# Making layer 1's masks, constant rows and first keys inside layer 0, with per-group slots and a second load of x in layer 0

## The chip, the core and the metric

The kernel runs on one core of a Trainium2 chip. The metric is the device time of one execution in microseconds (us); lower is better. Engines are named as in the profile: PE is the matrix engine (PEld its weight loads), DVE the vector engine, ACT the scalar engine, POOL the GpSimd engine, SP the queue that issues nearly all transfers (SPq in the timeline).

## The reference

Sixteen batches (B = 16) of 512 tokens with 256 features pass through two layers.

- Layer 0 attention: layer norm of x, queries from x, keys and values from the context; 16 heads of 16 features, rotary positions, and each query sees the 65 context positions that end at its own. Softmax, output projection, added to x.
- Layer 0 feed-forward: a gated recurrence over the batches (`c = f*c + i*g`, with gates from the normalized x of the batch and from `c`), sixteen steps, one for each batch. Its result is `h = tanh(x_n @ wo.T + c_final @ uo.T + bo)`, so every batch needs the state after the last one. `x = x + h`.
- Layer 1 attention: layer norm of x, full attention of 512 queries over 1601 context positions with a mask row for each batch. `x = x + attention`.
- Layer 1 feed-forward: eight experts, two for each token with limited room, a 256-1024-256 network with exact gelu.

```python
x = x + L0_xattn(layernorm(x), ctx, ctx)
x = x + L0_ffn(layernorm(x))       # recurrence over the 16 batches, then h for all
x = x + L1_xattn(layernorm(x), ctx, ctx, mask)
x = x + L1_ffn(layernorm(x))       # experts
```

## The kernel before

All tensors are fp32. The program has three blocks, one behind the other: layer 0 (`l0`), layer 1's attention (`l1`), the experts (`l2`). In each block the order of instructions is written by hand: every piece of work is put in a list by `at(when, fn, ...)`, the list is sorted by `when`, and the functions are called in this order. Each engine, and SP, then works through its own instructions strictly in this order; semaphores that the framework sets make it wait for what an instruction needs. A tile has `bufs` buffers that are used in turn, and a new tile waits until the old content of its buffer is no longer read. When a block ends, its tile pools are released and the next block's pools take over that memory.

**Layer 0** (lines 128 to 573). One step of the list is one unit of `when`; a batch takes `T0 = 32` steps, and batch b starts at `s0 = 32*b`. Pieces of several batches lie side by side: loads of batch b at s0-60, key and query projections at s0-49 to s0-35, rotation (`rope`, on POOL, then stores to DRAM in a layout with 32 rows per head) at s0-46 to s0-32. `slot` loads keys (s0-32) and queries (s0-26) back as four head groups at once, in halves `m` of two groups. For each head group g, `maxima` finds row maxima (s0-14+8g), `shift` brings their negatives through DRAM into a spare row of the query tile (s0-8+8g), `scores` and `values` follow (s0+8g). With `s1 = s0+32`, `recip_a` (s1+3) and `recip_b` (s1+6) send the softmax denominators and their reciprocals through DRAM (`raw_d` to `den`, `rec_d` to `rb`), `divide` (s1+10, POOL), `out_proj` (s1+13), `stats` and `finish` (normalization, s1+17), `turn` (transposes, s1+21), `gate` (s1+25) and `step` (s1+36) follow. `add_bias` (POOL, s0-40) adds the folded output bias to the batch's x tile, which is held in one of four buffers from load to `finish`. After the last job `uo` is applied to the final state (L559) and the bias row is added with a one-row matmul (L566).

**Layer 1 attention** (lines 576 to 1280). First the weights are loaded (L586), then constant rows are written into the DRAM tensors `ke_d` and `qe_d` (L621, L624), then the mask is loaded, turned into a keep row and a bias row and stored (L626 to L644). Then a loop over steps n from -84: a batch has `PER = 52` steps (4 head groups x 13 key chunks). `score` and `value` run from n = 0; `max_pair` (row maxima, PE L913 and DVE L921) runs `LEAD = 18` steps ahead. The keys of batch b are made ahead of it: `mask_rows`, `load_k`, `project_k` (PE L801, DVE L808), `mean_k`, `fill_k` (POOL L833), `add_k` (DVE L845), `halve_k` (L851, and L745/L748, which split the keys into a high and a low part), `store_k` (L857). For batch 0 these steps lie at n = -81 to -29, together with `load_x` (L691), `hidden` (L702), `stats`, `norm2`, `turn`, `project_q` (L755) and `store_q` (L770, L772), all of batch 0; the first `max_pair` of batch 0 needs `load_ks` (L893) and `load_qs` (L897), which read what these stored.

Of the kernel before, what the change touches and what calls it, by code (L numbers as in the profile page):

```python
# [2 lines left out]

# [8 lines left out]
F32 = mybir.dt.float32  # L12
# [45 lines left out]
def tile_kernel(ctx: ExitStack, tc: tile.TileContext, a, out):  # L58
# [68 lines left out]

    with ExitStack() as l0:
# [14 lines left out]

        def load(b):
            ctxT = pool.tile([P, 2, S], F32, name="ctxT")
            nc.sync.dma_start(out=ctxT, in_=a["ctxT"][b, :, :, 0:S])
            x_t = pool.tile([P, NQ, D], F32, name="x_t", bufs=4)
            nc.sync.dma_start(out=x_t, in_=a["x"][b])
            state[b] = {"x": x_t, "ctx": ctxT}
# [12 lines left out]
        zero = wp.tile([P, S], F32)  # L162
# [15 lines left out]
        wo0 = weight("wo0", [P, 2, D])  # L178
        gates = weight("gates", [P, 6, 2, D])
        uo = weight("uo", [P, 2, D])  # L180
        bo = wp.tile([P, D], F32)
# [7 lines left out]
        def clear(c):  # L189
            nc.sync.dma_start(  # L190
                out=flat[:, 2 * c * DS : 2 * (c + 1) * DS],
                in_=empty.rearrange("p r d -> p (r d)"),
            )

# [26 lines left out]
        def turn(key, b, k):  # L221
            if k == 0:
                state[b][key] = pool.tile([P, 2, S], F32, name=key)
# [50 lines left out]
        def slot(b, what, m):  # L274
            if m == 0:
                state[b][what] = pool.tile([P, NG, S], F32, name=f"{what}T")
            t_d = (k_d if what == "k" else q_d)[b % 2]
            nc.sync.dma_start(
                out=state[b][what][:, 2 * m : 2 * m + 2, :],
                in_=t_d[2 * m : 2 * m + 2].rearrange("g p n -> p g n"),  # L280
            )
# [23 lines left out]
        def maxima(b, g, half):  # L305
            qT, kT = state[b]["q"], state[b]["k"]
# [4 lines left out]
            for i in range(2):  # L311
                q = 2 * half + i
                lo = WIN if q == 0 else 0
                for j in range(4):
# [3 lines left out]
                        lhsT=qT[r0 : r0 + 32, g, q * P : (q + 1) * P],  # L318
                        rhs=kT[r0 : r0 + 32, g, q * P - WIN + lo : (q + 1) * P],
# [19 lines left out]
        def shift(b, g):  # L339
# [8 lines left out]
                out=state[b]["q"][HD:P:32, g, :],  # L348
# [7 lines left out]
        def scores(b, g, half):  # L356
            qT, kT = state[b]["q"], state[b]["k"]
            sc = [head_tile() for j in range(4)]
            for i in range(2):
                c = 2 * half + i  # L360
                w = width_of(c)
                for j in range(4):
# [3 lines left out]
                        lhsT=kT[r0 : r0 + 32, g, c * P : (c + 1) * P],  # L366
                        rhs=qT[r0 : r0 + 32, g, c * P : c * P + w],
# [41 lines left out]
        def recip_a(b):  # L409
# [5 lines left out]
            comp = pool.tile([P, 2, S], F32, name="comp")  # L415
# [91 lines left out]
        for b in range(B):  # L507
# [3 lines left out]
            for m in range(2):  # L511
                at(s0 - 49 + 2 * m, project, b, "k", m)
                at(s0 - 46 + 2 * m, rope, b, "k", m)
                at(s0 - 32 + m, slot, b, "k", m)
# [3 lines left out]
                at(s0 - 26 + m, slot, b, "q", m)  # L518
# [4 lines left out]
            at(s0 - 40, add_bias, b)  # L523
            for g in range(NG):
                for half in range(2):
# [6 lines left out]
            at(s1 + 6, recip_b, b)  # L532
            at(s1 + 10, divide, b)
            for p in range(2):
                at(s1 + 13 + 2 * p, out_proj, b, p)
# [11 lines left out]
        for c in range(E * CAPP // P // 2):  # L547
            at(7 * c, clear, c)
        jobs.sort(key=lambda x: (x[0], x[1]))
# [4 lines left out]
        for p in range(2):  # L554
            ps = bank()
            for i in range(2):
                q = 2 * p + i
                for k in range(2):
# [5 lines left out]
                        stop=False,  # L564
                    )
                nc.tensor.matmul(  # L566
                    ps[:, i * D : (i + 1) * D],
                    lhsT=one_row,
                    rhs=rows[:, RFO : RFO + D],
                    start=False,  # L570
                    stop=True,
                )
            nc.vector.tensor_copy(cu[:, 2 * p : 2 * p + 2, :].rearrange("p q d -> p (q d)"), ps)


    with ExitStack() as l1:
# [12 lines left out]
        wfo = weight1("wfo", [P, 2, D])  # L589
        wq1 = weight1("wq1", [P, 2, D])  # L590
        wk1 = weight1("wk1", [P, 2, D])
# [3 lines left out]

        ke_d = [dram.tile([NG, P, SKP], F32, name=f"ke_d{i}") for i in range(2)]  # L600
        qe_d = [dram.tile([NG, P, S], F32, name=f"qe_d{i}") for i in range(2)]
        ks_d = [dram.tile([H // 2, P, SKP], F32, name=f"ks_d{i}") for i in range(2)]
        qs_d = [dram.tile([H // 2, P, S], F32, name=f"qs_d{i}") for i in range(2)]
        raw_d = [dram.tile([NG, P, S], F32, name=f"raw1_d{i}") for i in range(2)]
        rec_d = [dram.tile([H, S], F32, name=f"rec_d{i}") for i in range(2)]
        m_d = dram.tile([B, SKP], F32, name="m_d")
        mb_d = dram.tile([B, SKP], F32, name="mb_d")
        rcnt = wp.tile([P, B], F32)
        bo = wp.tile([P, D], F32)


        with tc.tile_pool(name="mask", bufs=1) as mp:
            mask_i = mp.tile([B, SKP], I32)
            nc.sync.dma_start(out=mask_i, in_=a["mask"])
            kf = mp.tile([P, SKP], F32)
            nc.gpsimd.tensor_copy(kf, cols[:, KROW : KROW + 1].to_broadcast([P, SKP]))
            qf = mp.tile([P, S], F32)
            nc.gpsimd.tensor_copy(qf, cols[:, QROW : QROW + 1].to_broadcast([P, S]))
            for t in ke_d:
                for g in range(NG):  # L620
                    nc.sync.dma_start(out=t[g], in_=kf)  # L621
            for t in qe_d:
                for g in range(NG):
                    nc.sync.dma_start(out=t[g], in_=qf)  # L624
            keep = mp.tile([B, SKP], F32)
# [901 lines left out]
```

## Time and profile before

| | us |
|---|---|
| median of 3 runs (5949.54 to 5960.73) | 5958.36 |
| the profiled execution, its own device time | 5928.76 |
| span in the profile | 5926.7 |
| PE busy | 5555.2 (94%) |
| DVE busy | 3412.7 (58%) |
| ACT busy | 2632.9 (44%) |
| POOL busy | 1709.7 (29%) |
| last matmul of layer 0 starts | 1313.1 |
| first `max_pair` of layer 1 starts | 1461.3 |
| first `score` of layer 1 starts | 1535.7 |

The profile is one execution. Times in it are counted from the start of its span, and "busy" is time in which an engine runs an instruction. In a line of the timeline the columns are: start, duration, engine, line of the kernel, operation, output<-inputs by the program's names, shapes, xcount; in brackets the idle time of the engine before it and what ended that.

### The profile page before, as it was taken

How to read it: one execution, taken by the hardware profiler on the slowest of the kernel's cores; microseconds unless marked ns; L12 is line 12 of the kernel's file. 1: busy time of each engine (PE TensorE's matmuls, PEld its weight loads, DVE VectorE, ACT ScalarE, POOL GpSimd, SP SyncE). 2: the span in 40 equal slices, each digit the busy share in tenths (PEclk: the TensorE clock that was granted, in tenths of full speed). 3: DMA queues.
4: the chain of work that ended last, by engine and by line, in shares of the span. 5: the costliest groups of instructions: out<-in, count | busy, mean ns of one | idle time of the engine just before them, and what ended most of it. 6: DMA issues, size and time to landing. Idle time of an engine off the chain costs nothing. (4 is left out here: it accounts for less than half of the span.)

```text
span 5926.7 us, 95832 instructions
## 1 busy us (share of the span) xinstructions
PE 5555.2 (94%) x36560; PEld 2746.7 (46%) x36560; DVE 3412.7 (58%) x9204; ACT 2632.9 (44%) x5250; POOL 1709.7 (29%) x1322
## 2 busy tenths in 40 slices
PE   7999999963999999999999999999999987999999
PEld 4555555531433343333343334334334334766776
DVE  4555555522777777777777777777777741111111
ACT  3444444420355555555555555555555551222121
POOL 4555555322112222122122222313212012222222
PEclk7899898876899999999999999999999998999999
DMA  4333333324454555445445455544544412222211
GB/s 162 118 116 110 114 116 116 104 89 160 139 186 161 171 168 174 169 157 187 151 165 193 160 174 171 172 162 157 185 151 165 132 58 79 69 77 70 65 62 46
DMA packets 343773, 797.92 MB, mean 135 GB/s; under 512 B 46109, under 2 KB 124113, under 8 KB 341138
## 3 DMA queue, kind: packets, MB, share of 16 engines
q1 hardware_dynamic: 324114, 743.72, 37.3%
q0 software_dynamic: 19200, 48.08, 2.3%
q8 instruction: 288, 4.72, 0.3%
q14 instruction: 171, 1.40, 0.1%
HBM read 471.09 MB, written 326.73 MB: 135 GB/s over the span
## 5 line engine op out<-in xcount | busy, mean ns | idle before, releaser
L921 DVE TENSOR_REDUCE pm<-m 128x1 f32<-128x402 f32 (+1 forms) x4096 | 2125.8, 569 | 625.8 <-PE m L913 605.5
L1160 ACT ACTIVATE pt<-e 128x512 f32<-128x512 f32 (+1 forms) x3328 | 1715.9, 602 | 1155.4 <-PE e L1151 1154.2
L913 PEld LDWEIGHTS m<-ks,qs 64*128 64x128 f32 x4096 | 465.9, 186 | 1370.8 <-DVE pm L921 862.4
L913 PE MATMUL m<-ks,qs 64*128 64x402 f32 (+1 forms) x4096 | 1031.3, 452 | 17.2 <-DVE pm L921 14.7
L1151 PE MATMUL e<-qe,ke 32*128 32x512 f32 x6656 | 980.2, 643 | 0.0
L1173 PE MATMUL pv<-pt,vt 128*32 128x256 f32 (+2 forms) x9656 | 976.6, 476 | 0.0
L1354 ACT ACTIVATE hT<-h,cols 128x384 f32<-128x384 f32 (+1 forms) x320 | 199.2, 623 | 753.9 <-PE h L1346 736.3
L1374 PE MATMUL y<-w,hT 128*128 128x256 f32 x2176 | 476.3, 379 | 0.0
L1346 PE MATMUL h<-xeT,w 128*128 128x384 f32 (+1 forms) x1280 | 475.6, 530 | 0.0
L328 DVE CUSTOM_DVE_ANT_0 tmp<-s,cst 128x192 f32<-128x192 f32 (+1 forms) x1024 | 278.9, 336 | 320.1 <-PE s L316 318.9
L1374 PEld LDWEIGHTS y<-w,hT 128*128 128x128 f32 x2176 | 410.4, 190 | 54.4
L1151 PEld LDWEIGHTS e<-qe,ke 32*128 32x128 f32 x6656 | 271.2, 179 | 259.9 <-issue 220.6
L379 DVE TENSOR_TENSOR pt<-s,cst 128x384 f32<-128x384 f32 (+2 forms) x768 | 248.6, 392 | 178.4 <-PE s L364 178.4
L1346 PEld LDWEIGHTS h<-xeT,w 128*128 128x128 f32 x1280 | 243.8, 191 | 213.4 <-issue 114.9
L380 ACT ACTIVATE pt<-pt 128x384 f32<-128x384 f32 (+2 forms) x768 | 244.5, 390 | 190.2 <-DVE pt L379 189.9
L1173 PEld LDWEIGHTS pv<-pt,vt 128*32 128x32 f32 (+1 forms) x9656 | 191.4, 108 | 247.0 <-issue 245.0
L1386 POOL DMA_INDIRECT out<-y_t,xe x136 | 135.1, 994 | 590.8 <-DVE y_t L1383 586.0
L1331 DVE COPY xeT<-tp 128x384 f32<-128x384 f32 (+1 forms) x80 | 45.2, 606 | 446.4 <-PE tp L1328 446.4
L801 PE MATMUL m<-ck,wk 128*128 128x400 f32 (+1 forms) x512 | 215.0, 545 | 90.0 <-DMA ck<-in_ctxT 84.4
L1132 POOL DMA_INDIRECT slots<-row,put x128 | 132.9, 1039 | 571.9 <-issue 477.2
L833 POOL TENSOR_SCALAR u<-m_bc,kmean 128x802 f32<-128x802 f32 x64 | 192.0, 3000 | 327.6 <-DVE kmean L824 308.1
L106 POOL TENSOR_TENSOR rs<-mo,mhalf 128x4 f32<-128x4 f32 x64 | 66.4, 1038 | 691.7 <-DVE mo L104 691.5
(189 smaller groups left out, 5534.0 us busy)
## 6 DMA issues: line engine op xcount, KB each, us to landing
ks<-ks_d SPq DMA_DIRECT2D x128, 802.0 KB
ks_d<-khi SPq DMA_DIRECT2D x128, 401.0 KB
ks_d<-klo SPq DMA_DIRECT2D x128, 401.0 KB
ke<-ke_d SPq DMA_DIRECT2D x64, 802.0 KB
raw_d<-raw SPq DMA_DIRECT2D x128, 256.0 KB
qs<-qs_d SPq DMA_DIRECT2D x64, 512.0 KB
ck<-in_ctxT SPq DMA_DIRECT2D x64, 402.0 KB
ke_d<-kc SPq DMA_DIRECT2D x64, 401.0 KB
```

What stands on the lines that cost most here:

```text
L328: nc.vector.tensor_tensor_reduce(out=tmp[:, lo:], in0=sc[j][:, i, lo:BW], in1=band[:, lo:], scale=1.0, scalar=NEG, op0=ALU.add, op1=ALU.ma ...
L379: nc.vector.tensor_tensor(t, sc[j][:, i, 0:w], c, ALU.min)
L380: nc.scalar.activation(t, t, AF.Exp)
L801: nc.tensor.matmul(ps[:, 0:n], lhsT=wk1[:, k, m * P : (m + 1) * P], rhs=ck[:, k, 0:n], start=(k == 0), stop=(k == 1),)
L913: nc.tensor.matmul(sc[:, 0:n], lhsT=qs[r0 : r0 + 64, jp, q * P : (q + 1) * P], rhs=ks[r0 : r0 + 64, k0 : k0 + n], start=True, stop=True,)
L921: nc.vector.tensor_reduce(pms[b, g][:, q, 2 * jp + jj, part : part + 1], sc[:, 0:n], AX.X, ALU.max)
L1151: nc.tensor.matmul(sc[0:kn, :], lhsT=kt[r0 : r0 + 32, c * P : c * P + kn], rhs=qt[r0 : r0 + 32, :], start=True, stop=True,)
L1160: nc.scalar.activation(pt[0:kn, :], sc[0:kn, :], AF.Exp)
L1173: nc.tensor.matmul(pv[32 * j : 32 * j + 32, part], lhsT=vts[c // 2][0:kn, c % 2, v0 : v0 + 32], rhs=probs[b, g, c, j][0:kn, part], start=f ...
L1346: nc.tensor.matmul(ps[:, 0:n], lhsT=weights[e][0][:, k, m * P : (m + 1) * P], rhs=xeT[:, k, 0:n], start=(k == 0), stop=(k == 1),)
L1354: nc.scalar.activation(hT[:, m, 0:n], ps[:, 0:n], AF.Gelu, bias=cols[:, at : at + 1])
L1374: nc.tensor.matmul(ps[:, 0:D], lhsT=hT[:, m, t * P : (t + 1) * P], rhs=weights[e][1][:, m, :], start=(m == 0), stop=(m == NH - 1),)
```

## The change

Three things are done. (1) `ke_d`, `qe_d`, `ks_d`, `qs_d`, `m_d`, `mb_d`, `rcnt` and the weights `wk1`, `wfo`, `wq1` are made at the top of the kernel, so that layer 0 can use them. In layer 0's list, `masks` makes the mask rows at step 0 (on 64 partitions instead of 16), `constant_rows` writes the constant rows at steps 12 to 96, and the first batch's keys are made at steps 460 to 514 with the functions of `key_pieces`, which layer 1 uses for the other batches. (2) Memory in layer 0: `slot` loads each head group by itself at s0-20+8g, with four buffers of one group for keys and queries each, the x tile has two buffers and is loaded a second time at s1+7, with `add_bias` behind it at s1+11, and `xT`, `x1T`, `comp` and `zero` have fewer buffers. (3) Smaller ones: the bias of `uo` is added by DVE from a broadcast row (`b_out`) instead of four one-row matmuls, layer 1's `fold_bias` goes into its list at -61.5, and layer 1's value tiles are cleared on POOL instead of DVE.

The functions of `key_pieces` are those of layer 1 before, renamed; only what differs is shown.

```diff
+    first_weights = [const.tile([P, 2, D], F32, name=f"{n}_w") for n in ("wk1", "wfo", "wq1")]
+    def key_pieces(pool, bank, bufs):
+        def mask_rows(b):                      # before: m_bc
+            st[b, "keep"] = pool.tile([P, SKP], F32, name="keep", bufs=1)
+            nc.sync.dma_start(out=st[b, "keep"], in_=m_d[b : b + 1, :].to_broadcast([P, SKP]))
+        def load(b, m, i):                     # before: ck, [P, 2, 402]
+            c0, n = parts[i]
+            ck = pool.tile([P, 2, S], F32, name="ctxT")
+            nc.sync.dma_start(out=ck[:, :, 0:n], in_=a["ctxT"][b, :, :, c0 : c0 + n])
...
     with ExitStack() as l0:
+        def load_x(b):
+            x_t = pool.tile([P, NQ, D], F32, name="x_t")
+            nc.sync.dma_start(out=x_t, in_=a["x"][b])
+            state[b]["x"] = x_t
         def load(b):
             ctxT = pool.tile([P, 2, S], F32, name="ctxT")
             nc.sync.dma_start(out=ctxT, in_=a["ctxT"][b, :, :, 0:S])
-            x_t = pool.tile([P, NQ, D], F32, name="x_t", bufs=4)
-            nc.sync.dma_start(out=x_t, in_=a["x"][b])
-            state[b] = {"x": x_t, "ctx": ctxT}
+            state[b] = {"ctx": ctxT}
+            load_x(b)
...
         wo0 = weight("wo0", [P, 2, D])
+        for w, name in zip(first_weights, ("wk1", "wfo", "wq1")):
+            nc.sync.dma_start(out=w, in_=a[name])
...
+        b_out = wp.tile([P, D], F32)
+        nc.sync.dma_start(out=b_out, in_=a["rows"][:, RFO : RFO + D].to_broadcast([P, D]))
...
+        krow = wp.tile([P, SKP // 4], F32)
+        nc.gpsimd.tensor_copy(krow, cols[:, KROW : KROW + 1].to_broadcast([P, SKP // 4]))
+        (qrow likewise)
+        def constant_rows(i, g):
+            for t_d, row in ((ke_d, krow), (qe_d, qrow)):
+                nc.sync.dma_start(
+                    out=t_d[i][g].rearrange("p (r n) -> p r n", r=4),
+                    in_=row[:, None, :].to_broadcast([P, 4, row.shape[-1]]),
+                )
+        def masks():
+            n = 4 * B
+            mask_i = wp.tile([n, SKP // 4], I32)
+            nc.sync.dma_start(out=mask_i, in_=a["mask"].rearrange("b (r n) -> (b r) n", r=4))
+            ... (DVE: cast, not_equal; store m_d; count; own = ident summed by fours; dg = own*count)
+            nc.tensor.matmul(ps[:, 0:B], lhsT=ones[0:n, :], rhs=dg, start=True, stop=True)
+            ... (DVE: qscale, rcnt, two small reductions, bias row; store mb_d)
...
-        def slot(b, what, m):
-            if m == 0:
-                state[b][what] = pool.tile([P, NG, S], F32, name=f"{what}T")
-            t_d = (k_d if what == "k" else q_d)[b % 2]
-            nc.sync.dma_start(out=state[b][what][:, 2 * m : 2 * m + 2, :],
-                in_=t_d[2 * m : 2 * m + 2].rearrange("g p n -> p g n"))
+        def slot(b, g):
+            for what, t_d in (("k", k_d), ("q", q_d)):
+                t = pool.tile([P, S], F32, name=f"{what}T", bufs=4)
+                nc.sync.dma_start(out=t, in_=t_d[b % 2][g])
+                state[b][what, g] = t
...
-                at(s0 - 32 + m, slot, b, "k", m)
-                at(s0 - 26 + m, slot, b, "q", m)
-            at(s0 - 40, add_bias, b)
             for g in range(NG):
+                at(s0 - 20 + 8 * g, slot, b, g)
...
             at(s1 + 6, recip_b, b)
+            at(s1 + 7, load_x, b)
             at(s1 + 10, divide, b)
+            at(s1 + 11, add_bias, b)
...
+        at(0, masks)
+        for i in range(2 * NG):
+            at(12 + 12 * i, constant_rows, i // NG, i % NG)
+        keys = key_pieces(pool, bank, {"kc": 1, "k": 1})
+        at(460, keys.mask_rows, 0)
+        for m, o in ((0, 474), (1, 496)):
+            for i in range(4):
+                at(o + 2 * i - 3, keys.load, 0, m, i)
+                at(o + 2 * i, keys.project, 0, m, i)
+            at(o + 7, keys.mean, 0, m)
+            for h in range(2):
+                at(o + 8 + 5 * h, keys.fill, 0, m, h)
+                at(o + 10 + 5 * h, keys.add, 0, m, h)
+                at(o + 11 + 5 * h, keys.halve, 0, m, h)
+                at(o + 13 + 5 * h, keys.store, 0, m, h)
...
-                nc.tensor.matmul(ps[:, i * D : (i + 1) * D], lhsT=one_row,
-                    rhs=rows[:, RFO : RFO + D], start=False, stop=True)
-            nc.vector.tensor_copy(cu[:, 2 * p : 2 * p + 2, :].rearrange("p q d -> p (q d)"), ps)
+            nc.vector.tensor_add(cu[:, 2 * p : 2 * p + 2, :],
+                ps.rearrange("p (q d) -> p q d", q=2), b_out[:, None, :].to_broadcast([P, 2, D]))
     with ExitStack() as l1:
-        wfo = weight1("wfo", [P, 2, D])        (and wq1, wk1)
-        with tc.tile_pool(name="mask", bufs=1) as mp:   (the whole block, L612 to L645)
...
-            nc.vector.memset(t, 0.0)           (the seven vt tiles, L654 and L655)
+            nc.gpsimd.memset(t, 0.0)
...
-            at(s0 - 81, mask_rows, b)
+            if b:
+                at(s0 - 81, keys.mask_rows, b)
...
+                if b == 0:
+                    continue                   # keys of batch 0 are there already
+        at(-61.5, lambda: fold_bias(pool, bank(), bo, BV1, wo1, RO1))
```

## The prediction

> **What bounds the kernel now.** I read the page's strip of 40 slices first.
>
> ```profile
> PE   7999999963999999999999999999999987999999
> PEclk7899898876899999999999999999999998999999
> ```
>
> PE is nearly full everywhere but at the start, in slices 9 and 10 (about 1200 to 1500 us, where layer 0 hands over to layer 1) and near 5000. The chain that ended last covers only the experts' final 90 us and says nothing of this. So the busy times by stretch come next (columns: stretch, length, busy time and count of PE, PEld, DVE, ACT, POOL, then granted clock, DMA share, GB/s): a usual stretch of layer 0, and the handover cut at its events.
>
> ```profile
> 544.00:618.00 74.00, 65.98 (x562) 38.88 (x566) 37.25 (x190) 30.44 (x74) 39.23 (x29) 0.86 0.38 116
> ...
> 1310.00:1350.00 40.00, 8.76 (x19) 4.82 (x18) 8.48 (x19) 0.00 (x0) 2.30 (x3) 0.50 0.72 276
> 1350.00:1400.00 50.00, 12.28 (x32) 6.84 (x32) 14.95 (x37) 1.26 (x2) 20.88 (x12) 0.64 0.51 164
> 1400.00:1461.30 61.30, 19.34 (x40) 9.02 (x41) 10.87 (x21) 1.07 (x2) 11.06 (x5) 0.64 0.49 167
> 1461.30:1535.70 74.40, 70.10 (x149) 37.99 (x149) 52.27 (x113) 3.02 (x5) 21.46 (x13) 0.59 0.45 153
> ```
>
> Layer 0 is PE's (66 of 74 us a batch). From 1310 to 1461 no engine works half the time: a chain. The timeline shows its links.
>
> ```profile
> 1303.68 1.22 PE L566 MATMUL x<-rows,ones 1*128 1x256 f32 x2
> 1313.24 0.34 SPq L586 DMA_DIRECT2D wfo<-in_wfo  x1
> 1358.97 0.59 SPq L691 DMA_DIRECT2D x_t<-x_d  x1
> 1392.87 13.89 SPq L788 DMA_DIRECT2D ck<-in_ctxT  x3
> 1412.54 1.98 PE L755 MATMUL m<-xT,wq 128*128 128x512 f32 x4 [0.24 <-ACT xT L739]
> 1440.62 1.88 SPq L770 DMA_DIRECT2D qe_d<-qc  x1
> 1456.85 0.38 SPq L897 DMA_DIRECT2D qs<-qs_d  x1
> 1461.31 1.07 PE L913 MATMUL m<-ks,qs 64*128 64x402 f32 x3 [0.31 <-DMA qs<-qs_d]
> ```
>
> SP's first transfer of layer 1 starts with layer 0's last matmul: the pools are handed over only then. x is fetched 46 us later, behind the constant rows (1316.5 to 1335.8), the mask and four key loads; batch 0's query projection waits behind its second half of keys (PE stood until 1400.8 for `ck`); the queries' store waits on SP behind 20 us of key stores.
>
> Last, a batch of layer 0, where transfers end waits too.
>
> ```profile
> 587.75 1.18 SPq L412 DMA_DIRECT2D den<-raw_d  x1
> 595.86 0.55 DVE L422 RECIPROCAL den<-den 128x64 f32<-128x64 f32 x1 [3.84 <-DMA den<-raw_d]
> 597.80 2.20 PE L364 MATMUL s<-qT,kT 32*128 32x192 f32 x14 [3.60 <-DVE nm L328]
> 605.75 1.27 POOL L437 TENSOR_TENSOR comp<-comp,rb 128x512 f32<-128x512 f32 x1 [10.27 <-DMA rb<-rec_d]
> 607.08 1.22 PE L445 MATMUL x<-wo,comp 128*128 128x256 f32 x2 [1.79 <-POOL comp L437]
> ```
>
> The denominators take 8 us to come; DVE waits in order, and PE behind it. From 100 to 1200 the waits charge PE with 52.3 us for `comp` and 14.3 for scores behind DVE.
>
> **The change, the handover.** I rebuild the chain after the change in the same clock. The final state is ready at 1301.68 (L559 starts). Four L559 groups without the four one-row matmuls (1.15 each, by starts 1303.68 and 1304.83) take 4 x 2.0: 1309.8; the last add, as L711's, 0.69: 1310.5 (it was 1313.2 for SP). Three weights at 0.43 of SP: 1311.8; x and its transposed form landed within 5.8 before (1358.97 to L702 at 1364.76): 1317.6. `hidden` at the cold duration of a later one, 2 x 3.78: 1325.2. Then DVE's hs 0.69, and `fold_bias`, now queued between hs and `stats` on DVE, 3.5 (L116 at 1344.60 to L125 at 1348.12): 1329.4; ACT's tanh and POOL's add (0.63 + 1.26) lie beside it. `stats` 2.4, pow and normalization on POOL 6.0 (1381.66 to 1387.66), transposes and copies 2.0, projection cold 3.78: 1343.6, `qc` 0.8: 1344.4. From the first store of queries to the first `max_pair` it took 20.7 (1440.62 to 1461.31), with batch 1's mask row and key loads in between as they will be again; I leave 2 off for the key stores that no longer stand in the rings: 1363. **Gain 98.** Bounds: 108, with stores and loads at half (10 us); 85, if batch 1's loads (2 MB ahead of the queries' stores in the rings) hold them fully.
>
> Moved to POOL, the seven clears run from 1310.5; POOL's memset of 512 columns took 0.52 (L163), DVE's of 576 took 0.54 (L654), so some 5.5 us, hidden by the wait for x until POOL's first add at about 1326; without this cover 5.5. The 74 us from first `max_pair` to first `score` stay: 88 reductions of 0.49, batch 1's keys and values, none of it touched.
>
> **The first keys in layer 0.** PE: 8 projections at 1.58 (L801, four instructions at full clock) = 12.6. DVE: 8 x 0.66 + 0.6 + 4 x 1.05 + 4 x 0.57 = 12.4. POOL: 4 x 2.99 + 4 x 1.74 = 18.9. SP: 29 issues of 0.6 to 1.5. Step 474 is near 1168, 496 near 1206 (from the raw stores L404 at 1194 and 1206). PE is full from 1160 to 1200 (39.2 of 40), so the first half's 6.3 are on the path; from 1200 to 1250 PE idles 11 of 50, so the second half is partly covered. The rest is waits: POOL's fills stand ahead of `divide` and the state update of batch 14, DVE's `add` waits for POOL, and `maxima` and `scores` wait behind that for PSUM. L845 took 1.05 alone and 2.65 beside POOL's L748 (1420.1), so I add 5. **+18**, bounds 8 (half hidden) and 35 (all three engines' work half exposed).
>
> **The rest of layer 0.** Masks at step 0: `mask_i` landed in 3.9 (1316.00 to 1319.94); DVE's rows, a quarter as long, some 3; PE's matmul and answer 1.3. DVE waits in order, PE waits with its matmul, SP with two stores, and `shift` of the next group is queued behind them: **+6** once (2 to 12). Start: four more loads (0.9 MB, 4 issues of 0.65) ahead of the rotated keys' stores at 21.5, which POOL's pace hides mostly: **+2** (0 to 5). Constant rows: 8 x 1 MB at 350 GB/s (an estimate: 276 at a share of 0.72 and 164 at 0.51 make 383 and 322 for a full one), 3 us of backlog each, in steps with 14 us of slack: **+2** (0 to 8); they cost nothing unless `shift` or `recip` is just due.
>
> Slots by group take 1 MB of keys away from steps 0 and 1, just ahead of `den`, and 1 MB of queries from step 6 and 7, just behind `rb`, and put 0.5 MB at steps 4, 12, 20, 28. At 350 GB/s `den` comes some 3 us sooner, so DVE's stall (3.84) mostly ends; `rb` follows. Of 66.6 us of such waits I take 28 as recovered. Against this `add_bias` (2.34) now stands in POOL's queue behind `divide` and ahead of a normalization, the adds of `po` and a second normalization; POOL idled 4.8 us before the latter (622.7), so most is covered: +10 over 15 batches, and 35 without cover. The second load of x (512 KB) is behind `rb`, four steps before its use. **-18**, bounds -50 (most waits gone) and +25 (no gain from DMA order, POOL uncovered in most batches).
>
> A rule of the Trainium skill speaks against this part: DMA: Bandwidth & Descriptors, in Rules for kernel authors and Latency and other measured facts, wants transfers of 1 MiB or more, and puts a fixed cost near 2 us on each. By it the four extra loads a batch would be 4 x 2 x 16 = 128 us if they stood on the path, an estimate from that page, and the kernel would lose.
>
> By the rows a slot load is 0.44 of SP (L278), and the shortest trip through DRAM, `nm_d` to the query tile, waited 1.4 us (582.62 to 584.04); four more loads are 1.8 us of SP a batch, and each is due six steps (14 us) before use. I take zero; 28 (1.8 x 16) if SP were the bound.
>
> **Sum.** -98 + 18 + 6 + 2 + 2 - 18 = -88. The profiled execution has 5926.7 of span and 5928.76 of device time: it would be 5841. The median of the runs shown is 29.6 higher, 5958.36, without a cause in the profile; taken from it: **5870**.
>
> **Rivals.**
>
> *Layer 0 gains more:* the DMA order frees all 66 us of waits and the keys hide. Then -108 + 8 + 2 - 50 = -148: 5810. For it speak the 8 us that `den` takes; against it, that PE is busy 67 of 74 anyway and other waits come forward. 0.07.
>
> *The gain is mostly given back in layer 0,* by the keys at their upper price (35), masks 12, slots and bias at +25: -98 + 35 + 12 + 8 + 5 + 25 = -13: 5945. 0.12, and a third of it falls within the band of no change.
>
> *Slower: the second load of x stalls POOL.* `add_bias` waits in order for x; behind it stand two normalizations, the `po` adds and the next keys' rotation, and PE waits for all of them. If x, issued near 603, needs as long as `den` (8.1), it lands at 611.4, and POOL, done with `divide` at 609.5, loses 1.9 + 2.34 = 4.2 a batch. Without the gain from DMA order the rest is -98 + 28 = -70, so it decides from 4.4 us a batch (70 over 16) that no cover takes off; at 6, a landing of 10 us behind a full ring, the sum is -70 + 96 = +26: 5984. Against it: POOL idles 10.3 us before `divide` and 4.8 before the second normalization, and SP's longest wait for a transfer in layer 0 is 8.3. 0.07.
>
> *The change doesn't do what it says:* the handover is not bound by the keys but by the query chain and the pools' release. That is in my sum already: 50 of the 148 us remain.
>
> **How the numbers follow.** Forecast 0.74, rivals 0.07, 0.12 and 0.07. About 0.2% (12 us) is what can be told from no change. Faster 0.74 + 0.07 + 0.08 = 0.89, same 0.04, slower 0.07. The range goes from -136 (5822), near the first rival's end where all low bounds meet, to -38 (5920), where the handover is at 85, the keys at 35 and slots and bias cancel (-85 + 35 + 10 + 2); beyond it lie most of the two last rivals, less than 2 in 10.
>
> **What would show it.** In the new profile: x is fetched within 3 us of layer 0's last DVE add; the first L913 follows layer 0's last matmul by about 50 us instead of 148; the first `score` follows that by 74 still; layer 0's last matmul is at 1320 or so (+18 + 10 - 18); DVE's wait for `den` falls below 1 us, POOL has no wait for x before `add_bias`. Wrong would be: a batch of layer 0 over 76 us; PE waiting for `comp` or `x_n` more than the 4 us a batch of before; or queries' stores held by batch 1's loads so that the first L913 comes after 75 us.

## The result

| | before, us | after, us |
|---|---|---|
| median of 5 runs each | 5954.57 (5938.67 to 5960.73) | 5910.23 (5894.14 to 5913.07) |
| profiled execution, device time | 5928.76 | 5913.07 |
| span in the profile | 5926.7 | 5911.3 |
| final state ready (L559, now L744, starts) | 1301.68 | 1382.07 |
| first transfer of layer 1 (`wfo`, now `wv`) | 1313.24 | 1388.90 |
| first `max_pair` of layer 1 | 1461.31 | 1435.40 |
| first `score` of layer 1 | 1535.68 | 1508.21 |

The ratio of after to before is 0.9925, interval 0.9905 to 0.9945: 44 us faster by the medians. The forecast was 5870, its range 5822 to 5920.

The two profiled executions differ by 15.4 us of span, and this splits at two events: the state is ready 80.4 us later, from there to the first `max_pair` it takes 53.3 us instead of 159.6 (106.3 less), and from there to the end 10.5 us more. The last part is work that the change does not touch; over all profiles of this study it took 4461 to 4485 us without an order that the edits explain. So differences of single times below some 12 us mean little here, and the readings below go by landmarks ahead of it. Before's own five runs scatter over 22 us, and its profiled execution is below all of them, which is why the medians give 44 and the profiles 15. The 29 runs of before that were taken beside the experiments have medians of 5939.87 to 5942.45; against these, after's 5910.23 would be 30 to 32 us faster.

The page's strip of the kernel after (slices of 147.8 us):

```profile
PE   6888898976999999999999999999999987999999
PEclk7898988886999999999999999999999998999999
```

The hole of before (slices 9 and 10 at 6 and 3, in tenths of busy time) is now 7 and 6, but of the seven slices from the second on, all 9 before, five are now 8. The busy times by stretch say the same (columns as in the prediction): a usual batch, the last batches of layer 0, the handover, and the stretch from first `max_pair` to first `score`.

```profile
542.00:619.00 77.00, 66.18 (x587) 39.05 (x578) 37.98 (x189) 32.95 (x75) 37.36 (x29) 0.91 0.36 115
...
1235.00:1321.00 86.00, 58.22 (x416) 33.92 (x404) 32.29 (x114) 20.56 (x52) 34.74 (x20) 0.77 0.45 147
1321.00:1389.00 68.00, 37.74 (x88) 20.12 (x88) 6.81 (x15) 6.46 (x10) 21.17 (x14) 0.74 0.13 47
1389.00:1435.40 46.40, 21.53 (x46) 11.79 (x47) 7.01 (x22) 2.43 (x4) 16.64 (x24) 0.66 0.45 157
1435.40:1508.20 72.80, 67.81 (x146) 36.95 (x146) 52.22 (x113) 3.02 (x5) 21.48 (x13) 0.62 0.46 153
```

A usual batch takes 77 us with the same 66 us of PE: the added time is PE standing. From 1235 to 1321 PE idles 28 of 86 us, although the keys' matmuls are in it. From layer 1's first transfer to the first `max_pair` it is 46 us, where the forecast had about 50. Its links in the timeline of after:

```profile
1382.07 6.08 PE L744 MATMUL x<-uo,c_t 128*128 128x256 f32 x16 [7.34 <-POOL c_t L663]
1388.90 0.33 SPq L768 DMA_DIRECT2D wv<-in_wv  x1
1390.43 0.33 SPq L811 DMA_DIRECT2D x_t<-x_d  x1
1419.10 0.64 SPq L880 DMA_DIRECT2D qe_d<-qc  x1
1430.97 0.39 SPq L930 DMA_DIRECT2D qs<-qs_d  x1
1435.40 1.07 PE L946 MATMUL m<-ks,qs 64*128 64x402 f32 x3 [0.31 <-DMA qs<-qs_d]
```

x is fetched 1.5 us after layer 1's first transfer (45.7 before), and the queries' store comes 29 us after that (81.7 before, 1358.97 to 1440.62); nothing of batch 0's keys stands in between.

Where the 80 us went is read from the start of POOL's state update (`c_t<-gate`, L494 before, L663 after), one for each batch. Batch 0's is 17.0 us late (214.4 to 231.4), the twelve after it lose 15.4 more (910.2 to 925.6 from batch 0's to batch 12's), and the last three lose 48.0 (174.2 to 222.2 from batch 12's to batch 15's). I call these three the start, the steady stretch and the tail.

### The profile page after: what moved, and what is told of

The parts are those of the page before. It is cut to its first block, busy times and chain, and to the rows that moved or that the text cites. A ratio compares the mean times of both kernels' runs of the same rounds, so it can differ in the third digit from the quotient of the medians.

```text
span 5911.3 us, 95900 instructions
## 1 busy us (share of the span) xinstructions
PE 5548.7 (94%) x36550; PEld 2749.2 (47%) x36550; DVE 3397.3 (57%) x9190; ACT 2634.8 (45%) x5250; POOL 1715.3 (29%) x1336
## 5 line engine op out<-in xcount | busy, mean ns | idle before, releaser
L214 POOL TENSOR_SCALAR u<-keep,kmean 128x802 f32<-128x802 f32 x64 | 191.6, 2994 | 304.9 <-DVE kmean L205 286.5
L1419 DVE TENSOR_TENSOR y_t<-y,b 128x256 f32<-128x256 f32 x136 | 57.7, 424 | 359.0 <-PE y L1411 359.0
```

Of the source, the lines that this page charges most:

```text
L214: nc.gpsimd.tensor_scalar(u, st[b, "keep"][:, half_of(h)], 1.0, st[b, m, "mean"], ALU.subtract, ALU.mult)
```

## The experiments

All are edits of the kernel after. The theory is that the handover gained what was forecast, and layer 0 gave back 80 us in three places: in the tail through the bulk stores of the first keys, in the steady stretch through `add_bias` in POOL's order, at the start through the masks. The rivals are named in each expectation. They were run in groups, each beside the kernel before, whose medians were 5939.87 (13 runs; the first four experiments), 5942.45 (7 runs; two key buffers, keys in layer 1 with x held, keys spread, slots early), 5941.73 (9 runs; late bias, reload early, all together) and 5941.64 (1 run; no stores). In the table the columns are `c_t` of batch 0, from there to batch 12's, from there to batch 15's, two landmarks and the median time.

| kernel | c_t(0) | steady | tail | first transfer of layer 1 | first `max_pair` | time, median |
|---|---|---|---|---|---|---|
| before | 214.4 | 910.2 | 174.2 | 1313.2 | 1461.3 | 5954.57 |
| after | 231.4 | 925.6 | 222.2 | 1388.9 | 1435.4 | 5910.23 |
| after again | 235.2 | 924.3 | 219.3 | 1387.8 | 1436.1 | 5904.39 |
| keys in layer 1 | 235.7 | 916.4 | 177.7 | 1338.9 | 1457.7 | 5940.71 |
| masks early | 226.2 | 924.1 | 219.3 | 1378.8 | 1425.7 | 5899.78 |
| stores twice | 237.7 | 925.3 | 251.9 | 1424.7 | 1471.3 | 5942.52 |
| two key buffers | 232.4 | 923.3 | 223.4 | 1388.4 | 1434.9 | 5915.40 |
| keys in layer 1, x held | 228.6 | 896.4 | 174.9 | 1309.6 | 1428.6 | 5898.54 |
| keys in layer 1, x held, late bias | 232.3 | 911.1 | 176.4 | 1329.7 | 1449.8 | 5912.58 |
| keys spread | 235.3 | 938.7 | 176.9 | 1360.7 | 1407.4 | 5886.10 |
| slots early | 230.0 | 913.8 | 216.8 | 1369.7 | 1416.4 | 5887.48 |
| reload early | 234.2 | 895.2 | 215.1 | 1354.2 | 1400.9 | 5877.65 |
| no stores in the tail | 233.7 | 932.1 | 199.2 | 1374.1 | 1420.9 | 5884.24 |
| all together | 216.5 | 904.7 | 171.4 | 1301.6 | 1348.0 | 5824.82 |

**After again.** No edit.

> The changed kernel once more, to see how far one profile's landmarks repeat. If the loss in layer 0 is built into the schedule, the first c_t update of the state starts at 231 us again, batch 3's at 465, batch 12's at 1157, batch 15's at 1379, and layer 0's last matmul lies near 1389, each within 5 us. If part of the 76 us by which layer 0 ends later is a disturbance of that one execution, some of these landmarks move back towards those of the kernel before (214, 440, 1125, 1299) by more than 10 us.

Start, steady stretch and tail repeat within 4 us, the first `max_pair` within 1. The loss is built into the schedule. The kernels below give a measure of the scatter: in the seven profiles with the same work at the start `c_t(0)` lies between 231.4 and 237.7, and in the four that are the same up to batch 12 (after, the repeat, stores twice, two key buffers) the steady stretch lies between 923.3 and 925.6.

**Keys in layer 1.**

```diff
-        keys = key_pieces(pool, bank, {"kc": 1, "k": 1})
-        at(460, keys.mask_rows, 0)
-        ...
# layer 1's loop:
-            if b:
-                at(s0 - 81, keys.mask_rows, b)
+            at(s0 - 81, keys.mask_rows, b)
-                if b == 0:
-                    continue
```

> The first batch's keys are made at the start of layer 1 again; everything else is as in the changed kernel. Theory (the 48 us that layer 0 loses between batch 12 and batch 15 come from the keys): c_t of batch 0, 3 and 12 start where they do in the changed kernel (231, 465, 1157), batch 15's at about 1331 in place of 1379, the last matmul of layer 0 near 1340; the first of layer 1's maxima then lies 85 to 135 us behind that instead of 46.5. The keys' net worth is what the longer handover takes minus the 48 us: between 40 us slower and 10 us faster than the changed kernel. Rival (the tail is long for another reason, such as the reloading of x and the add_bias that have moved to the last steps): batch 15's c_t still starts near 1379.

The tail is 177.7: it is the keys that cost it, 42 us against the repeated kernel and 49 at layer 0's end. The 7 us between the two numbers lie in the steady stretch (916.4 against 924.3), ahead of the steps that the edit touches; why is open. The handover is then 119 us instead of 46 to 48, 70 to 72 more, still 29 short of before's 148. The ratio to before is 0.9993 (0.9978 to 1.0007): everything else in the change comes out at nothing (29 us gained in the handover, 26 lost by layer 0's end), and its whole gain is the move of the keys, 70 us in for 49 out, with the untouched rest's scatter on top.

**Masks early.**

```diff
+        mask_i = wp.tile([4 * B, SKP // 4], I32)           # ahead of gates
+        nc.sync.dma_start(out=mask_i, in_=a["mask"].rearrange(...))
-        at(0, masks)
+        at(-30, masks)
```

> The mask is loaded ahead of the gates' weights and the masks step stands at step -30 instead of 0. Theory (the in-order wait of DVE, PE and SP for the mask's load and sums costs 11 us at step 0): PE's wait at the masks' matmul falls from 10.9 us to under 3, c_t of batch 0 starts about 11 us earlier (220 instead of 231), all later ones too, and the time is about 11 us below the changed kernel's. Rival (the first batch waits for something else anyway, such as the round trip of q and k through DRAM): c_t of batch 0 stays at 228 to 231.

Timeline of after, PE, then the same line of this kernel:

```profile
87.03 0.57 PE L357 MATMUL x<-dg,ones 64*128 64x16 f32 x2 [10.89 <-DVE dg L355]
```

```profile
34.56 0.39 PE L357 MATMUL x<-dg,ones 64*128 64x16 f32 x2 [2.58 <-ACT rot L424]
```

The wait for the masks is gone, and c_t(0) comes 5 us (against after) to 9 us (against the repeat) earlier, not the full 11: other waits take part of it (from 20 to 235 us PE waits 16.1 us for its first context load and 10.0 for the first slots, against 13.4 and 7.6 in after). The whole schedule shifts by that, 9 to 10 us at layer 0's end. 5899.78 is 10 us below after, as expected, but within what the rest scatters.

**Stores twice.**

```diff
-            for r, t in ((0, hi), (2, hi), (1, lo), (3, lo)):
+            for r, t in ((0, hi), (2, hi), (1, lo), (3, lo)) * (1 if b else 2):
```

> The sixteen stores of the first batch's halved keys in layer 0 are issued twice each (the same data, 6.6 MB more or so); no other work is added. Theory (the stores' backlog in the DMA rings holds up the small round trips that layer 0's last batches need: nm_d, the denominators, the key loads): the stretch from batch 12's c_t to batch 15's grows by 15 to 40 us over the changed kernel's 222. Rival (the cost is the keys' matmuls and vector work on busy engines): it grows by less than 5 us, what the sixteen issues take on SP.

The tail grows by 32.6 us over the repeat (29.7 over after), where the rival allowed 5. But the edit does more than add bytes: each second copy goes to the same place as the first, and SP waits until the first has landed. The waits of SP from 1150 to 1430 us in this kernel (who waited on what, us in total, times, longest):

```profile
SPq L233 <- DMA ks_d<-khi: 16.3, 8, 5.0
SPq L233 <- DMA ks_d<-klo: 11.7, 8, 1.6
```

In after there are no such waits. These 28 us and the added bytes are not parted, so this run says little of the bytes; the run without stores, below, is the better test. How stores of 6.6 MB cost PE time is seen in the tail of after (timeline, SP, DVE and PE):

```profile
1243.83 1.25 SPq L233 DMA_DIRECT2D ks_d<-khi  x2
...
1248.80 0.37 SPq L515 DMA_DIRECT2D nm_d<-nmT  x1
1261.14 0.54 SPq L516 DMA_DIRECT2D qT<-nm_d  x1
...
1278.20 4.36 PE L183 MATMUL x<-ctxT,wk_w 128*128 128x402 f32 x8 [12.42 <-DMA ctxT<-in_ctxT]
...
1310.07 0.33 SPq L573 DMA_DIRECT2D raw_d<-raw  x1
...
1311.17 2.56 SPq L233 DMA_DIRECT2D ks_d<-khi  x2
1313.83 3.66 SPq L233 DMA_DIRECT2D ks_d<-klo  x2
1317.58 1.31 SPq L581 DMA_DIRECT2D den<-raw_d  x1
...
1325.44 0.55 DVE L591 RECIPROCAL den<-den 128x64 f32<-128x64 f32 x1 [7.00 <-DMA den<-raw_d]
...
1333.52 1.22 PE L614 MATMUL x<-wo,comp 128*128 128x256 f32 x2 [17.06 <-POOL comp L606]
```

The last raw store of batch 15 is issued at 1310.07, and `den`, which needs it, at 1317.58, behind five key stores: 7.5 us, against 2.05 for the same pair before (1237.82 to 1239.87). Two stores of `khi` took SP 1.25 us at 1243.83, the first of them all; here two take 2.56, and two of `klo` 3.66. Then comes the same trip as always (7.9 us to DVE's reciprocal), and PE stands 17 us. Earlier in the tail `nm_d`, stored behind four key stores, is fetched back only 12.3 us later (1248.80 to 1261.14), and behind the next four 6.1 (1273.96 to 1280.04); in the run without the stores these two trips took 7.7 and 2.3. SP waits for them, and the loads of the keys' context stand behind. With the stores doubled the same two waits of PE are (timeline, PE):

```profile
1297.63 5.70 PE L183 MATMUL x<-ctxT,wk_w 128*128 128x402 f32 x8 [20.41 <-DMA ctxT<-in_ctxT]
...
1368.39 1.22 PE L614 MATMUL x<-wo,comp 128*128 128x256 f32 x2 [32.48 <-POOL comp L606]
```

12.4 and 17.1 have become 20.4 and 32.5, with SP's waits for the first copies in them.

**Two key buffers.**

```diff
-        keys = key_pieces(pool, bank, {"kc": 1, "k": 1})
+        keys = key_pieces(pool, bank, {"kc": 1, "k": 2})
```

> Two buffers for each half of the keys (khi, klo) in layer 0 in place of one; nothing else. Theory (the DMA rings' backlog holds up layer 0's small round trips): POOL no longer waits 8 to 9 us for the landing of klo, but the same bytes stand in front of the same round trips, so the stretch from batch 12's c_t to batch 15's stays within 6 us of 219 to 222. Rival (the single buffers stall POOL and DVE, on which the batches' work queues): that stretch falls by 12 to 20 us and layer 0 ends as much earlier.

The tail stays at 223.4, though POOL's waits for the landing of `klo` (8.4 and 9.4 us in after) are gone. They were not on the path; what is left to explain the tail is the stores themselves, which the next run leaves out, and the work.

**No stores in the tail.**

```diff
-                at(o + 13 + 5 * h, keys.store, 0, m, h)
+            at(140 + 24 * i, stand_in, i)     # krow rows to ks_d[0][i], 8 of 821 KB
```

> The sixteen stores of the first batch's halved keys are left out of layer 0's tail (so the high and low parts that batch 0's maxima read are not its keys); eight transfers of the same total size write constant rows in their place from step 140 on, one each 24 steps. The keys' loads, projections, adds, splits and the slotted stores stay. Theory (the backlog of these stores is most of the tail's 49 us; doubled, they added 33): from batch 12's c_t to batch 15's it takes 185 to 195 us in place of 219, against 174 to 178 with no keys in layer 0. Rival (half the cost is the keys' loads and engine work, and the doubled stores only filled a ring that was not full before): 205 to 219.

The tail is 199.2, between the two ranges: neither expectation holds as written. The stores are worth 20 to 23 us, half of the tail's cost; the other half goes with what is left of the keys there, their loads, projections, sums and slotted stores, which were not parted further. PE's two waits in the tail show where the stores' half goes (timeline):

```profile
1279.24 2.99 PE L183 MATMUL x<-ctxT,wk_w 128*128 128x400 f32 x4 [4.98 <-DMA ctxT<-in_ctxT]
...
1319.30 1.22 PE L620 MATMUL x<-wo,comp 128*128 128x256 f32 x2 [9.25 <-POOL comp L612]
```

The wait for the last `comp` is 9.0 to 9.4 us in every kernel without these stores in the tail (9.42 before, 9.21 with the keys in layer 1, 9.25 here, 9.01 with the keys spread), and 16.9 to 17.7 in those that have them once (17.06 after, 16.86 in its repeat, 17.72 with two key buffers, 17.09 with the reload early): 8 us. The longest wait for `ctxT` falls from 12.4 to 5.0.

The eight transfers that stand in for them go with a steady stretch 7 us longer (932.1), about 1 us each.

**Keys spread.**

```diff
-        at(460, keys.mask_rows, 0)
-        for m, o in ((0, 474), (1, 496)):
+        at(FIRST - 10, keys.mask_rows, 0)     # FIRST = 255
+        for m in range(2):
+            o = FIRST + 96 * m
+            # load at o+10i, project at o+10i+7; half h: fill o+40+32h, add +4,
+            # split +5, stores in two parts at +8 and +21; "ck" as an own buffer
```

> The first batch's keys are still made in layer 0, but spread over six batches (steps 255 to 450) in place of the last two: one piece each ten steps, the stores of each half in two parts 13 steps apart, their own buffer for the context. Theory (bunching: 9 MB of stores and loads within 60 us delays round trips on which PE waits): the stretch from batch 12's c_t to batch 15's falls from 219 to 175 to 185 us, the batches 7 to 13 take 10 to 20 us more in all (the keys' 14 us of PE work and what their DMAs still collide with), layer 0 ends 25 to 35 us earlier, and the time is 25 to 35 us below the changed kernel's. Rival (the keys' cost is work and bytes, wherever they stand): the batches 7 to 13 take 40 to 50 us more, and the time stays within 10 us of the changed kernel's.

The tail is 176.9, as without keys; from batch 7 to batch 13 it takes 21 us more than before or than with the keys in layer 1 (446.3 and 446.6, now 467.7), just over what the theory allowed (10 to 20). Layer 0 ends 27 to 28 us earlier than in after, and the time is 24 us below after's; the ratio to before is 0.9901 (0.9876 to 0.9926). Against the kernel with the keys in layer 1, layer 0 ends 22 us later, where the bunch made it 49: the same work and bytes cost half when they do not come in one bunch.

**Keys in layer 1, x held** (in four buffers).

```diff
+            x_t = pool.tile([P, NQ, D], F32, name="x_t", bufs=4)
-            at(s1 + 7, load_x, b)
-            at(s1 + 11, add_bias, b)
+            at(s0 - 40, add_bias, b)
```

> The first batch's keys are back in layer 1, as in the run that had only that; moreover x is held in four buffers as in the kernel before, not loaded again, and add_bias stands 40 steps ahead of the batch again. Theory (reload and later add_bias cost about 7 us over the steady batches): from batch 0's c_t to batch 12's it takes 906 to 912 us as in the kernel before (910), against 916 with the reload. Rival (the slots per group and their waits cost it, or nothing does): 914 to 920 us again. If the reload had brought the 28 us that the prediction gave it, 935 us or more.

The steady stretch is 896.4, below every range expected: 20 us less than with reload and late `add_bias`, and 14 less than before. So something in the pair of reload and late `add_bias` costs 20 us, and the rest of the change shortens these batches; the slots by group are the part of it that was meant to, but were not tried alone. The next two part the pair.

**Keys in layer 1, x held, late bias.** As the last, with `add_bias` left at s1+11.

> The first batch's keys in layer 1 and x held in four buffers without a second load, as in the run that held x, but add_bias stays at s1+11. Theory (the place of add_bias on POOL costs it): from batch 0's c_t to batch 12's it takes 914 to 920 us as with the reload (916), DVE waits over 30 us for x_t. Rival (the second load costs it): 896 to 902 as with x held and add_bias early (896).

911.1: 15 of the 20 us come back with the place of `add_bias` alone, 5 with the second load (916.4). The theory's range is missed by 3 us and the rival's by 9; the place is the larger part. The theory's other sign holds: from 240 to 1120 us DVE waits 33.7 us for `x_t` behind the `po` adds (L624), where it waits 7.1 with `add_bias` early, and nothing else was changed between the two.

**Reload early.**

```diff
-            at(s1 + 7, load_x, b)
+            at(s0 + 21, load_x, b)
-            at(s1 + 11, add_bias, b)
+            at(s0 + 25, add_bias, b)
```

> The changed kernel with the second load of x at step s0+21 in place of s1+7 and add_bias at s0+25 in place of s1+11, 18 steps earlier; still two buffers for x. Theory (add_bias behind divide and ahead of the po adds in POOL's queue makes x_t late, which the wait of DVE's statistics for x_t shows: 36.6 us against 7.0): that wait falls to about 7 us, PE's wait behind nmT from 12 to 5, the stretch from batch 0's c_t to batch 12's from 924 to 900 to 908 us, layer 0 ends 15 to 28 us earlier and the time is as much lower. Rival (the second load of x itself, 512 KB more a batch, costs it): the stretch stays at 916 to 926.

895.2: with the second load kept and both 18 steps earlier, the steady stretch is 29 to 30 us shorter than in after and as short as with x held, so the second load costs nothing that is seen in this place, although POOL now stands at `add_bias` for 84 us in all, 30 of them charged to the load of x (240 to 1120 us). Layer 0 ends 34 us earlier, more than expected, since the tail is 4 to 7 us shorter too. The time is 5877.65, the ratio to before 0.9883 (0.9857 to 0.9910). POOL's order in after and DVE behind it (timeline):

```profile
632.52 1.26 POOL L606 TENSOR_TENSOR comp<-comp,rb 128x512 f32<-128x512 f32 x1 [0.69 <-DMA rb<-rec_d]
634.02 2.34 POOL L391 TENSOR_TENSOR x_t<-x_t,bo 128x1024 f32<-128x1024 f32 x1 [0.24 <-DMA x_t<-in_x]
...
642.26 2.50 POOL L624 TENSOR_TENSOR x_t<-x_t,po 128x512 f32<-128x512 f32 x2
643.58 0.43 DVE L101 BATCH_NORM_STATS2 st<-x_t 128x6 f32<-128x256 f32 x1 [2.89 <-POOL x_t L624]
```

And with the early reload:

```profile
619.95 1.26 POOL L606 TENSOR_TENSOR comp<-comp,rb 128x512 f32<-128x512 f32 x1 [0.83 <-DMA rb<-rec_d]
...
627.13 2.51 POOL L624 TENSOR_TENSOR x_t<-x_t,po 128x512 f32<-128x512 f32 x2
```

From the second `comp` to the `po` adds it is 9.7 us in after and 7.2 here; `add_bias` took its 2.34 out of that, and DVE waited 2.89 for `x_t`. The waits from 240 to 1120 us (columns: who waited on what, us in total, times, longest), first after:

```profile
PE x L614 <- POOL comp L606: 61.6, 24, 5.7
PE x L411 <- ACT nmT L514: 12.4, 12, 2.1
```

```profile
DVE st L101 <- POOL x_t L624: 36.6, 12, 3.8
```

then the early reload:

```profile
PE x L614 <- POOL comp L606: 49.3, 24, 4.4
PE x L411 <- ACT nmT L514: 5.1, 12, 0.4
```

```profile
DVE st L101 <- POOL x_t L624: 7.4, 12, 1.3
```

DVE's wait falls by 29 us, PE's two by 19.6, as the theory had it for DVE's and for the one behind nmT. PE's wait for `comp` is hardly touched by the place of `add_bias` alone (49.1 with x held and late bias, 47.9 with x held), so its part in the 19.6 has another cause, which is open.

**Slots early.**

```diff
-                at(s0 - 20 + 8 * g, slot, b, g)
+                at(s0 - 25 + 8 * g, slot, b, g)
```

> The loads of the slots stand five steps earlier (at -25 + 8g in place of -20 + 8g); nothing else. Theory (the trace names qT's load for four waits of PE of 1 to 4 us in the first batch, and for none of weight later): c_t of batch 0 starts 5 to 10 us earlier than 231 to 235 us, the stretch from batch 0's to batch 12's stays at 920 to 926 us, and the time falls by 5 to 10 us. Rival (later loads per group are what makes the steady batches 7 us slower): that stretch falls to 910 to 918 us. Against both: SP waits earlier for the slots' buffers and holds up the stores behind them, and the time rises.

c_t(0) is 1 to 5 us earlier, less than the theory had and hardly outside the scatter. But the steady stretch is 913.8, 11 us shorter: the rival's range, although no wait of weight is charged to the slots there. The time, 5887.48, is 23 us below after's, where the theory had 5 to 10. PE's wait for `comp` fell from 61.6 to 41.4 us in the same window; which transfer is spared by the earlier loads was not tried.

**All together.** Keys spread, masks early, slots early, reload early, and the constant rows every 32 steps.

> All that helped in one kernel: keys spread over steps 255 to 450, masks at step -30, slots five steps earlier, x's second load and add_bias 18 steps earlier, and the constant rows every 32 steps in place of 12. If the gains add up: c_t of batch 0 near 220 (9 us from the masks, 4 from the slots), the steady stretch to batch 12 some 20 us shorter than with the keys spread alone (939 to about 918), a clean tail of 177, layer 0's end near 1322 and the first of layer 1's maxima near 1369, and a time of 5835 to 5855, 55 to 75 us below the changed kernel. If the parts share their cover (POOL's queue and the rings), 5860 to 5885.

5824.82, ratio to before 0.9797 (0.9777 to 0.9817): 117 us below the kernel before, and 85 below after. The start is within 2 us of before, the steady stretch 5 us shorter than before with the keys in it, the tail 171.4, and layer 0 ends 12 us earlier than before. The handover stays at 46.3 us. The gain is larger than the sum expected, by 10 us of the lower end; the constant rows' spacing is in it, and its share was not taken by itself.

## Why the prediction was right and wrong

The sign was right, the median lay in the range, and the size was half. That the range held was partly luck: as a change it reached from -136 to -38, the profiles moved by -15, and only the medians of the first five runs each moved by -44. Term by term, against the profiled before:

| term | forecast | measured | from |
|---|---|---|---|
| handover, final state to first `max_pair` | -98 (-85 to -108) | -106 | 159.6 to 53.3 |
| first keys in layer 0 | +18 (8 to 35) | +42 to +49 | tail, and layer 0's end, against the run with the keys in layer 1 |
| start and masks | +8 (2 to 17) | +17 to +21 | c_t(0); masks 5 to 9 of it |
| constant rows, slots, x, `add_bias` | -16 (-50 to +33) | +14 to +15 | steady stretch |

The **handover** was right in its links: x within 3 us, 37.0 us from the final state to the first store of queries against 42.7 forecast (1301.68 to 1344.4), first `max_pair` 46.5 us after layer 1's first transfer against "about 50" after layer 0's last matmul, first `score` 72.8 after that against 74.

**The keys are one of the two steps that failed, by 24 to 31 us.** The working counted PE 12.6, DVE, POOL and "29 issues" on SP, put the engines' work on the path by halves, and gave 5 us to engines waiting for each other. It named the transfers but put their time at nothing in SP's order: 6.6 MB of stores within 75 us stand ahead of `den`, of `nm_d`'s return and of the context loads, and PE waits for these. The run without the stores shows it (tail 199 instead of 219 to 222, PE's wait for the last `comp` 9 us instead of 17). The issue times it took (0.6 to 1.5) were also short by rows of the profile before, where two stores of `klo` held SP for 3.86 us (1385.41). The upper bound of 35 was too low for the same reasons. The other half of the tail's cost, 20 to 25 us, is near the +18 forecast. DMA: Bandwidth & Descriptors of the Trainium skill, in Queues, rings and completion order, says that SP has one ring on each DMA engine and that descriptors are consumed there in ring order. `nm_d`'s trips of 12.3 and 6.1 us behind the key stores, 7.7 and 2.3 without them, agree with it. `den` was late because SP issued it late, and how much of the loss goes by either way was not parted.

**The place of `add_bias`** is the other. It was seen in its place ("behind `divide` and ahead of a normalization, the adds of `po`"), and priced at +10 with POOL's idle time of 4.8 us ahead of the second normalization as cover. The cover was real for POOL and not for DVE: its statistics wait in order for the `po` adds, and scores and maxima queue behind them (DVE's wait for `x_t` 36.6 us against 7.4). Its price with the reload was 29 to 30 us over twelve batches (the upper bound, without cover, was 35); by itself, with the keys in layer 1, it was 15. **Slots and DMA order** had the sign right: with that price gone the steady stretch is 15 us shorter than before (constant rows included) where 28 were forecast for all of layer 0; what of it is the slots was not parted. DVE's wait for `den` did fall, from 9.0 to 2.1 us (240 to 1120 us), but PE's for `comp` rose, from 45.6 to 61.6.

**Masks and start**: in the order of the forecast's upper bounds; 10.9 us of PE's wait stood in the profile where 6 were taken, and PE waited 3.9 us for the first slots (65.81, `qT<-q_d`), which the forecast had not seen for a pipeline that is still filling; the rest of the 17 to 21 us is not taken apart. **Constant rows** were not parted; some 8 us of the steady stretch are lost by batch 3, when they are written, and the stand-in stores' 1 us each make that plausible. With the early reload, though, these three batches take 225.8 us against 225.1 before, so at most part of the 8 is theirs.

Of the **rivals**, the one that has the gain mostly given back in layer 0 (+85 there, -13 in all) describes the profile better than the forecast does (+80, -15). It was given 0.12; the keys alone passed their upper bound. In the profiles' scale it said 5916 and the forecast 5841, and the profiled execution took 5913. In the medians' scale, with 29.6 us added to both, the rival is 35 us high and the forecast 40 low: the medians fell by more than the profiles did, and why before's unprofiled runs are slower than its profiled one is open. The rival with a second load of x that stalls POOL fell: POOL waited 1.5 us for x in all from 240 to 1120 us, and the load moved earlier costs nothing that is seen; the place of `add_bias`, which it also named, was the true part of it. By the figures that the prediction took from DMA: Bandwidth & Descriptors, four more loads a batch would cost an estimated 128 us if they stood on the path. They do not stand there: with them and the early reload the steady stretch is 15 us shorter than before.

Two of the three signs of being wrong that the prediction named are in the profile of after: a batch of layer 0 over 76 us (77.1), and PE waiting more than 4 us a batch for `comp` and `x_n` (5.8).

## What to carry to other kernels

When work is moved under cover, its transfers move too: count what its stores put ahead of each small round trip on the same queue, and spread bulk stores over many steps instead of the last gap before a hand-over. An instruction that hides in an engine's idle time can still delay the next engine's in-order queue; follow its consumer, not its own engine. After a move has paid less than it should, compare one recurring landmark per batch between the profiles: start, slope and tail point to different causes. When a store is doubled to test its price, look whether the second copy waits for the first.

## What the runs showed of the hardware

A key store that SP issues in about 0.6 us as the first of a bunch (1.25 for two at 1243.83) takes up to 2.0 us further on in the bunch (L233, 3.99 for two of `klo` at 1299.40), so the issuing queue itself becomes late, and with it transfers that share nothing with the stores but the queue (`den`, 7.5 us instead of 2.05). A second buffer for the stored tiles changed nothing (tail 223.4 against 222.2). A second store to the same place, issued by the same queue, waited for the first to land (28.0 us in 16 waits). Perfetto Trace Analysis of the Trainium skill (DMA Instruction, HWDGE) says that the span of such a row ends when the descriptors have been made and the issuing engine is free again, and that the movement itself is not in it. That fits: the 2.56 and 3.66 us are SP's, and `den`, whose row is 1.31 us, reached DVE only 7.9 us after its start.
